# Both heads' probabilities in one tile: one softmax-sum addition for two heads, split anew between GpSimd and VectorE

## The chip, the cores and the metric

The kernel runs on one core of one Trainium2 chip. The time is the device time of one execution in microseconds (us). The engines are named as in the profile: PE is TensorE (PEld its weight loads), DVE is VectorE, ACT is ScalarE, POOL is GpSimd, SP is SyncE, from whose queue nearly all DMAs start.

## The reference

Four transformer layers in fp32 on one sequence of 2048 tokens with 128 features, each with an attention and a feed-forward part and residuals. The change lies in the attention of the second layer, L1, with 16 heads of 64 features:

```python
q = jnp.einsum('bsd,dhk->bshk', x, Wq) + bq
k = jnp.einsum('bsd,dhk->bshk', x, Wk) + bk
v = jnp.einsum('bsd,dhk->bshk', x, Wv) + bv
q = q / jnp.sqrt(jnp.asarray(depth, q.dtype))
attn = jnp.einsum('bqhd,bkhd->bhqk', q, k)
attn = jax.nn.softmax(attn, axis=-1)
out = jnp.einsum('bhqk,bkhd->bqhd', attn, v)
return jnp.einsum('bqhd,hdm->bqm', out, Wo) + bo
```

The queries are normalised tokens. Before it comes L0 (16 heads of 8 features, then a feed-forward part); after it come the L1 feed-forward, L2 (a three-neighbour attention and eight experts, one per token) and L3 (a recurrent memory in chunks of 64 tokens, then eight experts, two per token, and a shared one).

## The kernel before

**Order of work.** Every engine runs its instructions in the order in which the program issues them. That order is made while the program is built: `note` keeps a model clock for each engine, with costs per instruction from `COST`, and `fill` puts small pieces of the work of the other stages (`parts` and `helpers`, written as generators) between the steps of the attention, when the model says that their inputs and a PSUM bank are ready. `leave` is the number of banks that such pieces must leave free. Nothing is reordered on the chip, so an instruction that comes late delays all that stands behind it on its engine.

**L1 attention.** The queries are cut into five blocks (`QB`) of 512, 388, 512, 384 and 256 columns (some blocks carry four spare or extra columns). A *unit* is one block and one pair of heads, so there are 5 x 8 = 40 units, and a unit has 16 *steps*, one for each 128 keys. `l1_attn` runs over the 640 steps. In a step:

- TensorE makes the scores of both heads (four products for each, row halves side by side) into two PSUM banks of pool `st`, of which there are three. A score is already lessened by the row's maximum.
- ScalarE writes exp of each head's scores to an SBUF tile `P` of 128 x 512, from pool `pp` with seven buffers (two tiles in each step).
- `max_upto` issues the row maxima of a later unit: TensorE multiplies keys `km` by queries `qh` into banks of pool `mx` (five banks), VectorE reduces each (`mx<-mi`). These reductions run ahead of the unit that needs them. A unit of 512 columns has a pair of them in each step; smaller ones have fewer.
- `fill` puts in pieces of other stages: the preparation of queries, the ends of units, and, as soon as a block's result is there, L1's feed-forward, L2 and L3. They take their banks from pool `mx` too.
- `do_sum` handles the step before: it adds that step's P to a running sum over the steps, which is the softmax denominator before its sum over partitions. Steps 14 and 15 (`dve=(14, 15)`) go to VectorE (sum `acd`), steps 0 to 13 to GpSimd (sum `acg`). The first tile of either engine is only remembered; the second makes the sum with an addition of two P tiles. So each unit and head has 13 additions on GpSimd and one on VectorE.
- `do_pv` multiplies P by the values (`mi<-P,ka`), one bank for both heads over the 16 steps.

After a unit's last step, `do_merge` adds `acg` to `acd` on VectorE, once for each head, and `u_end` follows as a piece: TensorE sums over partitions (`mi<-acd,ones`), four DMAs turn the row of sums for a reciprocal and spread it back, VectorE multiplies the result `o` by it (`o<-o,rb`), and every second unit adds to the output projection. The next unit's sums take the same buffers (`l1a`, two for each of `acd` and `acg`, one for each head).

**After the attention** the rest of L2 and L3 is issued (`drain`). The experts of L3 run in two lanes and, from here on, in five more, which borrow the attention's tiles: `lane_tiles` takes weights into `acd`, `acg` and `ka` tiles, `lane_work` takes one P tile of pool `pp` for each expert step and uses its two halves of 256 columns. L0's attention uses pool `pp` too, with tiles of one head.

In the profile nearly every instruction has the line of the helper that records it, L147, so groups are told apart by their tiles.

Of the kernel before, what the change touches and what calls it, by code (L numbers as in the profile page):

```python
# [28 lines left out]
CH = 64  # L29
NCH = S // CH  # L30
ATANH = (1.0000000039388743, 0.3333315796754013, 0.20012426861749952, 0.13980709417165652, 0.14087328632693624)
T = dict(lead0=22, more0=4, mgap=0.4, pvq=2, lim0=0.5, fq=(3,), pl=-0.5, pr=1.0, tlow=2, tback=3, late=0.3, pvp="mx", mxp="mx", ex=(1280, 1792, 2047), low=1, lows='ge', keep=1, leave=2, pvn=1, sp=0, rdy=40., eu=2, qg=(22, 16, 10), em=2, el=6, sem=0.2, same=1.2, tsame=3.0, order="hdmBbAaEcCeg", ps=dict(st=3, mx=5), dma=2.3, slack=0.1, lim=0.3, backlog=2.5, lead=(10, 8, 6), pp=7, dve=(14, 15), qp=(1, 1), lanes=2, xl=5,
         QB=[(0, 512, 512), (512, 384, 388), (896, 512, 512), (1408, 384, 384), (1792, 256, 256)])


# [35 lines left out]
def body(ctx: ExitStack, tc: tile.TileContext, x, pa, pb, pc, pi, pd, pr, pr0, pe, pw, out):  # L71
# [87 lines left out]
    ctx.enter_context(tc.manual_schedule(engines={ET.PE, ET.DVE, ET.Activation, ET.Pool}))  # L159
    sm = ctx.enter_context(tc.tile_pool(name="sm", bufs=3))  # L160
    tp = ctx.enter_context(tc.tile_pool(name="tp", bufs=2))
    pp = ctx.enter_context(tc.tile_pool(name="pp", bufs=T["pp"]))

    bank = dict(st=[0.0] * 3, pv=[0.0], mx=[0.0] * 3, bg=[0.0])
    owner = {}
# [352 lines left out]
    l0ctx = ExitStack()  # L518
    l0 = l0ctx.enter_context(tc.tile_pool(name="l0", bufs=1))
    l0w = l0ctx.enter_context(tc.tile_pool(name="l0w", bufs=2))  # L520
    qd = dram.tile([16, 6, 8, S], BF16, name="qd")
    kd = dram.tile([16, 6, 8, S], BF16, name="kd")

# [148 lines left out]
    def l0_attn():  # L672
# [49 lines left out]
        for g in range(N):  # L722
            h, j = divmod(g, 16)
            i = h % NKQ
            if j == 0:
                need(("m0", h))
                need(("ld", h))
            if j == 2 and h + 2 < H0:
                helper(("ld", h + 2), l0_load(h + 2))
            pts = []  # L730
            pss = []
            for q in range(4):
                if q == T["pvq"] and prev is not None:
                    do_pv(*prev)
                if not pss:

                    while min(bank["st"]) > clk["T"] + T["mgap"] and min(bank["mx"]) < min(bank["st"]) - T["mgap"] and \
                            done[0] < min(4 * N, 4 * (g + LEAD + T["more0"]) + q):
                        more_max()

                    two = done[0] == 4 * N and h >= H0 - 2 and q % 2 == 0
                    for e in range(1 + two):
                        pss.append(take(["st"]))
                        r = slice(LOW * e, LOW * e + NR0P + 2)
                        mm(pss[e], kop[i][r, j * 128:(j + 1) * 128], qop[i][r, (q + e) * 512:(q + e + 1) * 512],
                           par=e and 0.02)
                    if done[0] < 4 * N and done[0] <= 4 * (g + LEAD) + q:
                        more_max()
                ps = pss.pop(0)
                p = pp.tile([128, 512], F32, name="P", tag="P")  # L750
                se.activation(p, ps, AF.Exp, scale=1.0 / math.sqrt(HD0))
                rel(ps)
                pts.append(p)
                fill(T["lim0"], "t" if q not in T["fq"] else "")
            prev = (g, pts)
            emitted.add(("s0", g))
            yield g
# [192 lines left out]
    e0ctx.close()  # L950
    psum_pools(**T["ps"])
    in0[0] = False
    leave[0] = T["leave"]
    COST.update(L1COST)
    clk.update(dict.fromkeys("TADPS", 0.0))
    for d in (wr, rd, by, bank):
# [4 lines left out]
    l1 = ctx.enter_context(tc.tile_pool(name="l1", bufs=1, reuse_waits="tile"))  # L961
    kap = ctx.enter_context(tc.tile_pool(name="kap", bufs=3, reuse_waits="tile"))
    l1w = ctx.enter_context(tc.tile_pool(name="l1w", bufs=2, reuse_waits="tile"))
    l1a = ctx.enter_context(tc.tile_pool(name="l1a", bufs=2, reuse_waits="tile"))
    KC = 256
    opool = ctx.enter_context(tc.tile_pool(name="opool", bufs=3, reuse_waits="tile"))
    def u_loadk(u, c):
# [8 lines left out]
    def u_end(u, o, accs):  # L976
# [3 lines left out]
        t = mi()  # L980
        if u == len(units) - 1:
            for e in range(2):
                mm(t[64 * e:64 * e + 64, :n], ones[:, 0:64], accs[e][:, :n], par=(e == 1))
            yield
            rb = l1w.tile([128, 512], F32, name="rb", tag="rb", bufs=1)
            ve.reciprocal(rb[:, :n], t[:, :n])
            rel(t)
            ve.tensor_tensor(o[:, :n], o[:, :n], rb[:, :n], ALU.mult)
            O[p] = o
            yield from stage_wo(qb, NP1 // 2 - 1)  # L990
            return
        for e in range(2):
            mm(t[32 * e:32 * e + 32, :n], ones[:, 0:32], accs[e][:, :n], tile_position=(0, 32 * e), par=(e == 1))
        emitted.add(("s", u))
        yield
        sr = l1w.tile([128, 512], F32, name="rb", tag="rb", bufs=1)
# [69 lines left out]
    def l1_attn():  # L1066
# [15 lines left out]
        def do_pv(g, pts, v):  # L1082
            u, k = divmod(g, 16)
            n = QB[units[u][0]][2]
            if k == 0:
                pv[u] = take([T["pvp"]])
            for e in range(2):
                mm(pv[u][64 * e:64 * e + 64, :n], v[:, k % SPC, 64 * e:64 * e + 64], pts[e][:, :n],
                   start=(k == 0), stop=(k == 15), par=(e == 1))
            if k == 15:  # L1090
                accs = acc.pop(u)
                if u:
                    need(("o", u - 1))
                o = opool.tile([128, 512], F32, name="o", tag="o")
                se.copy(o[:, :n], pv[u][:, :n])
                rel(pv.pop(u))
                ends.append((u, o, accs))

        def do_sum(g, pts, v):
            u, k = divmod(g, 16)  # L1100
            n = QB[units[u][0]][2]
            for e in range(2):
                a = acc.setdefault(u, [None, None])
                f = first.setdefault((u, e), {})
                eng, nm = (ve, "d") if k in T["dve"] else (ge, "g")
                if nm not in f:
                    f[nm] = [pts[e]]
                    continue
                if len(f[nm]) == 1:
                    if u:  # L1110
                        need(("s", u - 1), ("o", u - 1))
                    t = l1a.tile([128, 512], F32, name="ac" + nm, tag="ac" + nm)
                    eng.tensor_tensor(t[:, :n], f[nm][0][:, :n], pts[e][:, :n], ALU.add)
                    f[nm] = [t, 1]
                else:
                    t = f[nm][0]
                    eng.tensor_tensor(t[:, :n], t[:, :n], pts[e][:, :n], ALU.add)
                if k == 15:
                    a[e] = f["d"][0]
                    merge.append((f["d"][0], f["g"][0], n))  # L1120
                    del first[(u, e)]

        merge = []

        def do_merge():
            while merge:
                d, g_, n = merge.pop(0)
                ve.tensor_tensor(d[:, :n], d[:, :n], g_[:, :n], ALU.add)
            while ends:
                u, o, accs = ends.pop(0)  # L1130
                helper(("o", u), u_end(u, o, accs), max(wr[tname(t)] for t in accs))

        ends = []
        prev = []
# [1 line left out]
        for g in range(16 * U):  # L1136
# [15 lines left out]
            if k % SPC == 0:  # L1152
                ka, v = nxt.pop(0)
                g2 = g + 2 * SPC
                if g2 < 16 * U:
                    nxt.append(u_loadk(g2 // 16, (g2 % 16) // SPC))
            pts = []
            ks = slice((k % SPC) * 128, (k % SPC) * 128 + 128)
            pss = [take(["st"]) for _ in range(2)]
            ops = ((ka[:, 0, ks], qhh[u]), (ka[:, 0, ks], qlt[u % 2]), (ka[:, 1, ks], qhh[u]), (onr, mbt[u % 2]))  # L1160
            for i, (a, b) in enumerate(ops):
                for e in range(2):
                    rows = slice(64 * e, 64 * e + 64)
                    mm(pss[e][:, :n], a[rows], b[rows, :n], start=(i == 0), stop=(i == 3), par=e and 0.02)
            for e in range(2):
                pt = pp.tile([128, 512], F32, name="P", tag="P")
                se.activation(pt[:, :n], pss[e][:, :n], AF.Exp)
                rel(pss[e])
                pts.append(pt)
            max_upto(max_at(g + 16 + LEAD[n] + 1))  # L1170
            fill()
            if prev:
# [655 lines left out]
    def lane_tiles(lane):  # L1828
# [4 lines left out]
        if lane not in lane_bufs:  # L1833
            n = lane - LANES
            if n < 2:
                t = ("acd", "acg")[n]
                ws = [l1a.tile([128, 512], F32, name=t, tag=t)[:, :384] for _ in range(2)]
                r = l1x.tile([128, 512], F32, name="qf", tag="qf")
            else:
                t = kap.tile([128, 3, KC], F32R, name="ka", tag="ka").rearrange("p a b -> p (a b)").bitcast(F32)  # L1840
                ws = [t[:, :384], t[:, 384:768]]
                r = kmp.tile([128, 512], F32R, name="km", tag="km").bitcast(F32)
            lane_bufs[lane] = [(w.rearrange("p (a m) -> p a m", a=3), r[:, BN * i:BN * i + BN])
                               for i, w in enumerate(ws)]
# [3 lines left out]
    def lane_work(lane):  # L1848
        if lane < LANES:
            return bt(f"t3{lane}", 1), bt(f"te{lane}", 1)  # L1850
        p = pp.tile([128, 512], F32, name="P", tag="P")
        return p[:, :BN], p[:, BN:]

    def e_load(lane):

# [262 lines left out]
```

## Time and profile before

| What | Value |
|---|---|
| Three runs | 2988.46, 2989.47, 3006.5 us; median 2989.47 |
| Profiled execution | 3001.08 us, span of the profile 2999.2 us |
| Busy, share of the span | PE 92%, DVE 73%, ACT 53%, POOL 51% |
| Granted TensorE clock, mean | 0.936 |
| First L1 exponential, last one's end | 909 us, 2595 us |
| GpSimd additions `acg<-acg,P` and `acg<-P` | 960 and 80, 1011.4 and 91.1 us busy |
| VectorE additions `acd<-P`, merges `acd<-acd,acg` | 80 and 80 |
| VectorE maxima `mx<-mi`, L0 and L1 | 2080, 1322.1 us busy |

A line of the profile's groups names the engine, the operation, the tiles (result, arrow, inputs), the shape, the number of instructions, their busy time and mean, and the idle time of the engine before them with what ended it. The table by stage gives the busy time of every engine in a stretch. A timeline line has the start, the length and the instruction; equal instructions in a row are one line (x2, x4), and a bracket at the end is the idle time before it and what ended it. "mi" is a PSUM bank.

### The profile page before, as it was taken

How to read it: one execution, taken by the hardware profiler on the slowest of the kernel's cores; microseconds unless marked ns; L12 is line 12 of the kernel's file. 1: busy time of each engine (PE TensorE's matmuls, PEld its weight loads, DVE VectorE, ACT ScalarE, POOL GpSimd, SP SyncE). 2: the span in 40 equal slices, each digit the busy share in tenths (PEclk: the TensorE clock that was granted, in tenths of full speed). 3: DMA queues.
4: the chain of work that ended last, by engine and by line, in shares of the span. 5: the costliest groups of instructions: out<-in, count | busy, mean ns of one | idle time of the engine just before them, and what ended most of it. 6: DMA issues, size and time to landing. Idle time of an engine off the chain costs nothing.

```text
span 2999.2 us, 49776 instructions
## 1 busy us (share of the span) xinstructions
PE 2769.9 (92%) x16719; PEld 1307.0 (44%) x16719; DVE 2194.9 (73%) x4699; ACT 1582.9 (53%) x3933; POOL 1522.3 (51%) x1762
## 2 busy tenths in 40 slices
PE   7999999999979899999999999899989898888998
PEld 2222222322234344454444444455544555565666
DVE  7899898898534666566666778887677769787765
ACT  1788887888854444444444444444434334333444
POOL 2400110201127688866776876677767556443444
PEclk9999999999979999999999999999999999776779
DMA  6311231321144333433442332233334343312244
GB/s 142 72 28 22 72 84 17 101 54 46 53 141 135 92 112 110 121 110 111 138 119 87 94 95 87 89 105 108 109 97 114 108 117 94 88 52 61 76 104 115
DMA packets 247749, 275.80 MB, mean 92 GB/s; under 512 B 95747, under 2 KB 183330, under 8 KB 247366
## 3 DMA queue, kind: packets, MB, share of 16 engines
q1 hardware_dynamic: 246630, 272.43, 33.2%
q8 instruction: 132, 2.16, 0.3%
q14 instruction: 123, 1.01, 0.1%
q10 hardware_dynamic: 864, 0.20, 0.0%
HBM read 229.97 MB, written 42.28 MB: 91 GB/s over the span
## 4 chain that ended last, share of the span: by engine, by line
PE 70%; DVE 18%; ACT 6%; issue 3%; DMA 3%; POOL 1%; SPq 0%; ACTq 0%; DVEq 0%; POOLq 0%
PE mi L147 70%; DVE mx L147 5%; ACT P L147 3%; DVE sB L147 1%; DVE o L147 1%; DVE gq L147 1%; DMA ka<-kvd 1%; DVE gt L147 1%; DVE xs L147 1%; ACT kf L147 1%; ACT kh L147 1%; DVE xn L147 1%; DVE sG L147 1%; DVE acd L147 1%; DVE sA L147 0%
## 5 line engine op out<-in xcount | busy, mean ns | idle before, releaser
L147 DVE TENSOR_REDUCE mx<-mi 128x1 f32<-128x512 f32 (+1 forms) x2080 | 1322.1, 683 | 582.8 <-PE mi L147 571.5
L147 ACT ACTIVATE P<-mi 128x512 f32<-128x512 f32 (+3 forms) x2304 | 1137.0, 551 | 1004.1 <-PE mi L147 973.2
L147 POOL TENSOR_TENSOR acg<-acg,P 128x512 f32<-128x512 f32 (+3 forms) x960 | 1011.4, 1083 | 181.8 <-ACT P L147 180.0
L147 PE MATMUL mi<-P,ka 128*64 128x512 f32 (+3 forms) x2560 | 597.6, 546 | 2.3 <-DVE mx L147 2.3
L147 PE MATMUL mi<-qh,ka 64*128 64x512 f32 (+3 forms) x2560 | 521.0, 406 | 9.7 <-DMA ka<-kvd 6.8
L147 PEld LDWEIGHTS mi<-qh,ka 64*128 64x128 f32 x2560 | 247.0, 189 | 382.5 <-issue 347.0
L147 PE MATMUL mi<-kop,qop 48*128 48x512 bf16 x1024 | 348.6, 405 | 24.5 <-DVE mx L147 12.1
L147 PE MATMUL mi<-qop,kop 50*128 50x512 bf16 x1024 | 317.8, 391 | 27.1 <-ACT P L147 24.7
L147 PE MATMUL mi<-P,vop 128*32 128x512 f32 x2048 | 304.3, 623 | 13.9 <-ACT P L147 13.9
L147 POOL TENSOR_SCALAR vep<-mv 128x2 f32<-128x2 f32 (+1 forms) x24 | 5.5, 229 | 495.6 <-DVE mv L147 495.6
L147 PE MATMUL mi<-km,qh 64*128 64x512 f32 x1024 | 225.6, 410 | 30.4 <-DVE mx L147 23.8
L147 PE MATMUL mi<-mbt,onr 64*128 64x512 f32 (+3 forms) x1280 | 228.7, 351 | 1.5 <-DMA mbt<-mb 1.5
L147 PE MATMUL mi<-ql,ka 64*128 64x512 f32 (+3 forms) x1280 | 229.2, 353 | 0.0
L147 PEld LDWEIGHTS mi<-P,ka 128*64 128x64 f32 x2560 | 129.2, 137 | 225.3 <-issue 195.1
L147 PEld LDWEIGHTS <-kop 50*128 50x128 bf16 x1024 | 63.6, 95 | 304.9 <-issue 281.6
L147 POOL TENSOR_TENSOR acg<-P 128x512 f32<-128x512 f32 (+3 forms) x80 | 91.1, 1158 | 202.5 <-DVE acd L147 162.0
L147 PEld LDWEIGHTS mi<-km,qh 64*128 64x128 f32 x1024 | 107.1, 189 | 60.5 <-DVE mx L147 38.5
L147 PEld LDWEIGHTS mi<-mbt,onr 64*128 64x128 f32 x1280 | 124.6, 190 | 13.9 <-DMA mbt<-mb 2.2
L147 PEld LDWEIGHTS mi<-ql,ka 64*128 64x128 f32 x1280 | 125.7, 192 | 0.0
L147 PEld LDWEIGHTS <-qop 48*128 48x128 bf16 x1024 | 72.9, 96 | 97.2 <-issue 82.7
L147 PEld LDWEIGHTS mi<-P,vop 128*32 128x32 f32 x2048 | 55.5, 109 | 119.8 <-issue 90.7
L147 POOL TENSOR_TENSOR kl<-kf,kh 128x512 f32<-128x512 f32 x32 | 40.9, 1278 | 110.9 <-ACT kh L147 82.4
(509 smaller groups left out, 3464.4 us busy)
## 6 DMA issues: line engine op xcount, KB each, us to landing
ka<-kvd SPq DMA_DIRECT2D x320, 384.0 KB
km<-khd SPq DMA_DIRECT2D x159, 256.0 KB
khd<-kh SPq DMA_DIRECT2D x32, 256.0 KB
kvd<-kh SPq DMA_DIRECT2D x32, 256.0 KB
kvd<-kl SPq DMA_DIRECT2D x32, 256.0 KB
kvd<-vt SPq DMA_DIRECT2D x16, 512.0 KB
ka<-in_pw_dram SPq DMA_DIRECT2D x37, 192.0 KB
w3s<-in_pw_dram SPq DMA_DIRECT2D x35, 192.0 KB
```

Of the source, the lines that this page charges most:

```text
L147: r = f(*a, **k)
```

## The change

One P tile now holds both heads of a step, 128 x 2 x 512, from a new pool of five buffers. ScalarE still writes each head with an instruction of its own, and TensorE still reads each head by itself. `do_sum` makes one addition over both heads, of twice the columns, and so does the merge; the sums are one tile for both heads (pool `l1a`, one buffer of each). VectorE takes steps 5, 6, 11 and 12 of a unit and GpSimd the other twelve, so a unit has 11 additions on GpSimd and three on VectorE, and one merge. L0 keeps its tiles of one head in a pool of its own that ends with L0. The number of banks that pieces leave free is one more from the end of a unit's P-by-values product to the start of the next. The lanes take the new tiles: five P buffers where there were seven, and halves of one `acd` or `acg` tile where there were two tiles.

```diff
-T = dict(lead0=22, ..., pp=7, dve=(14, 15), ...
+T = dict(pp1=5, lead0=22, ..., pp=7, dve=(5, 6, 11, 12), ...
...
-    pp = ctx.enter_context(tc.tile_pool(name="pp", bufs=T["pp"]))
...
+    l0p = l0ctx.enter_context(tc.tile_pool(name="l0p", bufs=T["pp"]))
...
-                p = pp.tile([128, 512], F32, name="P", tag="P")
+                p = l0p.tile([128, 512], F32, name="P", tag="P")
...
-    leave[0] = T["leave"]
+    leave[0] = T["leave"] + 1
...
-    l1a = ctx.enter_context(tc.tile_pool(name="l1a", bufs=2, reuse_waits="tile"))
+    l1a = ctx.enter_context(tc.tile_pool(name="l1a", bufs=1, reuse_waits="tile"))
+    pp = ctx.enter_context(tc.tile_pool(name="pp", bufs=T["pp1"], reuse_waits="tile"))
...
-            mm(t[32 * e:32 * e + 32, :n], ones[:, 0:32], accs[e][:, :n], tile_position=(0, 32 * e), par=(e == 1))
+            mm(t[32 * e:32 * e + 32, :n], ones[:, 0:32], accs[:, e, :n], tile_position=(0, 32 * e), par=(e == 1))
...
             if k == 0:
                 pv[u] = take([T["pvp"]])
+                leave[0] -= 1
...
-                mm(pv[u][64 * e:64 * e + 64, :n], v[:, k % SPC, 64 * e:64 * e + 64], pts[e][:, :n],
+                mm(pv[u][64 * e:64 * e + 64, :n], v[:, k % SPC, 64 * e:64 * e + 64], pts[:, e, :n],
...
                 rel(pv.pop(u))
+                leave[0] += 1
...
         def do_sum(g, pts, v):
             u, k = divmod(g, 16)
             n = QB[units[u][0]][2]
-            for e in range(2):
-                ...
-                    t = l1a.tile([128, 512], F32, name="ac" + nm, tag="ac" + nm)
-                    eng.tensor_tensor(t[:, :n], f[nm][0][:, :n], pts[e][:, :n], ALU.add)
-                ...
+            f = first.setdefault(u, {})
+            eng, nm = (ve, "d") if k in T["dve"] else (ge, "g")
+            if nm not in f:
+                f[nm] = [pts]
+            elif len(f[nm]) == 1:
+                if u:
+                    need(("s", u - 1), ("o", u - 1))
+                t = l1a.tile([128, 2, 512], F32, name="ac" + nm, tag="ac" + nm)
+                eng.tensor_tensor(t[:, :, :n], f[nm][0][:, :, :n], pts[:, :, :n], ALU.add)
+                f[nm] = [t, 1]
+            else:
+                t = f[nm][0]
+                eng.tensor_tensor(t[:, :, :n], t[:, :, :n], pts[:, :, :n], ALU.add)
+            if k == 15:
+                acc[u] = f["d"][0]
+                merge.append((f["d"][0], f["g"][0], n))
+                del first[u]
...
-                ve.tensor_tensor(d[:, :n], d[:, :n], g_[:, :n], ALU.add)
+                ve.tensor_tensor(d[:, :, :n], d[:, :, :n], g_[:, :, :n], ALU.add)
...
+            pts = pp.tile([128, 2, 512], F32, name="P", tag="P")
             for e in range(2):
-                pt = pp.tile([128, 512], F32, name="P", tag="P")
-                se.activation(pt[:, :n], pss[e][:, :n], AF.Exp)
+                se.activation(pts[:, e, :n], pss[e][:, :n], AF.Exp)
...
-                ws = [l1a.tile([128, 512], F32, name=t, tag=t)[:, :384] for _ in range(2)]
+                t = l1a.tile([128, 2, 512], F32, name=t, tag=t)
+                ws = [t[:, e, :384] for e in range(2)]
...
-        p = pp.tile([128, 512], F32, name="P", tag="P")
-        return p[:, :BN], p[:, BN:]
+        p = pp.tile([128, 2, 512], F32, name="P", tag="P")
+        return p[:, 0, :BN], p[:, 0, BN:]
```

More of the change, by code (lines that the diff above doesn't have):

```diff
@@ L31 @@
 ATANH = (1.0000000039388743, 0.3333315796754013, 0.20012426861749952, 0.13980709417165652, 0.14087328632693624)
-T = dict(lead0=22, more0=4, mgap=0.4, pvq=2, lim0=0.5, fq=(3,), pl=-0.5, pr=1.0, tlow=2, tback=3, late=0.3, pvp="mx", mxp="mx", ex=(1280, 1792, 2047), low=1, lows='ge', keep=1, leave=2, pvn=1, sp=0, rdy=40., eu=2, qg=(22, 16, 10), em=2, el=6, sem=0.2, same=1.2, tsame=3.0, order="hdmBbAaEcCeg", ps=dict(st=3, mx=5), dma=2.3, slack=0.1, lim=0.3, backlog=2.5, lead=(10, 8, 6), pp=7, dve=(14, 15), qp=(1, 1), lanes=2, xl=5,
+T = dict(pp1=5, lead0=22, more0=4, mgap=0.4, pvq=2, lim0=0.5, fq=(3,), pl=-0.5, pr=1.0, tlow=2, tback=3, late=0.3, pvp="mx", mxp="mx", ex=(1280, 1792, 2047), low=1, lows='ge', keep=1, leave=2, pvn=1, sp=0, rdy=40., eu=2, qg=(22, 16, 10), em=2, el=6, sem=0.2, same=1.2, tsame=3.0, order="hdmBbAaEcCeg", ps=dict(st=3, mx=5), dma=2.3, slack=0.1, lim=0.3, backlog=2.5, lead=(10, 8, 6), pp=7, dve=(5, 6, 11, 12), qp=(1, 1), lanes=2, xl=5,
          QB=[(0, 512, 512), (512, 384, 388), (896, 512, 512), (1408, 384, 384), (1792, 256, 256)])
@@ L982, in u_end @@
             for e in range(2):
-                mm(t[64 * e:64 * e + 64, :n], ones[:, 0:64], accs[e][:, :n], par=(e == 1))
+                mm(t[64 * e:64 * e + 64, :n], ones[:, 0:64], accs[:, e, :n], par=(e == 1))
             yield
@@ L1101, in do_sum @@
             n = QB[units[u][0]][2]
-            for e in range(2):
[L1103 to L1111, printed above, removed]
-                    t = l1a.tile([128, 512], F32, name="ac" + nm, tag="ac" + nm)
-                    eng.tensor_tensor(t[:, :n], f[nm][0][:, :n], pts[e][:, :n], ALU.add)
[L1114 to L1121, printed above, removed]
+            f = first.setdefault(u, {})
[15 more added lines that the diff above has]
+                del first[u]
         merge = []
@@ L1127, in do_merge @@
                 d, g_, n = merge.pop(0)
-                ve.tensor_tensor(d[:, :n], d[:, :n], g_[:, :n], ALU.add)
+                ve.tensor_tensor(d[:, :, :n], d[:, :, :n], g_[:, :, :n], ALU.add)
             while ends:
                 u, o, accs = ends.pop(0)
-                helper(("o", u), u_end(u, o, accs), max(wr[tname(t)] for t in accs))
+                helper(("o", u), u_end(u, o, accs), wr[tname(accs)])
         ends = []
@@ L1156, in l1_attn @@
                     nxt.append(u_loadk(g2 // 16, (g2 % 16) // SPC))
-            pts = []
             ks = slice((k % SPC) * 128, (k % SPC) * 128 + 128)
@@ L1164, in l1_attn @@
                     mm(pss[e][:, :n], a[rows], b[rows, :n], start=(i == 0), stop=(i == 3), par=e and 0.02)
+            pts = pp.tile([128, 2, 512], F32, name="P", tag="P")
             for e in range(2):
-                pt = pp.tile([128, 512], F32, name="P", tag="P")
-                se.activation(pt[:, :n], pss[e][:, :n], AF.Exp)
+                se.activation(pts[:, e, :n], pss[e][:, :n], AF.Exp)
                 rel(pss[e])
-                pts.append(pt)
             max_upto(max_at(g + 16 + LEAD[n] + 1))
```

## The prediction, made before the result was known

> **What bounds the kernel now.** I read the page first, for the shares; then busy time by stage, cutting the span at the first exponentials of each block of queries in the L1 attention (909 to 2595 us: 40 units of 16 steps, with blocks of 512, 388, 512, 384 and 256 columns); then the waits inside those stages; then the timelines where TensorE stood still.
>
> ```profile
> PE 2769.9 (92%) x16719; PEld 1307.0 (44%) x16719; DVE 2194.9 (73%) x4699; ACT 1582.9 (53%) x3933; POOL 1522.3 (51%) x1762
> ```
> ```profile
> core 0: us, PE busy (x) PEld busy (x) DVE busy (x) ACT busy (x) POOL busy (x), PEclk, DMA share, GB/s
> 909.00:1248.00 339.00, 330.12 (x1858) 142.99 (x1857) 199.21 (x301) 160.51 (x303) 271.08 (x236) 0.98 0.36 111
> 1248.00:1543.00 295.00, 290.21 (x1928) 147.15 (x1928) 189.69 (x347) 139.57 (x340) 213.58 (x216) 0.99 0.41 122
> 1543.00:1939.00 396.00, 376.62 (x2066) 169.56 (x2066) 307.46 (x556) 174.27 (x392) 289.64 (x250) 0.98 0.30 92
> 1939.00:2281.00 342.00, 326.22 (x2151) 171.92 (x2148) 246.18 (x519) 148.19 (x422) 235.78 (x273) 0.97 0.37 105
> 2281.00:2595.00 314.00, 283.96 (x2120) 162.85 (x2117) 243.94 (x608) 125.42 (x473) 191.63 (x292) 0.91 0.42 110
> 2595.00:2999.00 404.00, 344.46 (x1723) 256.64 (x1721) 289.38 (x1069) 160.11 (x660) 167.20 (x279) 0.76 0.31 79
> ```
>
> The first columns are the stretch and its length. TensorE sets the pace: in the five L1 stages it lacks only 8.9, 4.8, 19.4, 15.8 and 30.0 us of being always busy, 78.9 us in all. That is all that the change can win there. The engine it relieves, POOL, is not the bound; the engine it loads, DVE, is busy for 59, 64, 78, 72 and 78% of the stages.
>
> What makes the 78.9 us shows in one place:
>
> ```profile
> 971.82 10.90 DVE L147 TENSOR_TENSOR o<-o,rb 128x512 f32<-128x512 f32 x1
> ```
> ```profile
> 967.38 14.79 POOL L147 TENSOR_TENSOR acg<-acg,P 128x512 f32<-128x512 f32 x12
> ```
> ```profile
> 984.20 0.58 PE L147 MATMUL mi<-ident,m 128*4 128x128 f32 x2 [8.88 <-DVE m L147]
> ```
>
> A DVE product of two SBUF tiles, 0.66 us at its shortest, stays open for 10.90 us, until POOL's unbroken row of additions ends; the maxima queue behind it, and TensorE stands for 8.88 us. I followed each held DVE instruction of the five stages in the timelines of DVE and POOL. At the end of a POOL instruction with a pause after it, however short, DVE always got in (67 of 67); at an end with the next addition already running, 144 times of 208. TensorE's gaps behind single holds of over 2 us (o, gq, u, cc, sA) add up to 33.9 us.
>
> **What goes and comes, engine by engine.** The sums are against the profiled execution, 3001.08 us with a span of 2999.2, which is 0.4% above the median of the runs, 2989.47; I put the difference on the median.
>
> ```profile
> L147 POOL TENSOR_TENSOR acg<-acg,P 128x512 f32<-128x512 f32 x384 | 489.7, 1311 | 51.2 <-ACT P L147 51.0
> ...
> L147 POOL TENSOR_TENSOR acg<-acg,P 128x256 f32<-128x256 f32 x192 | 137.4, 738 | 57.4 <-ACT P L147 56.8
> ...
> L147 POOL TENSOR_TENSOR pbl<-vt,pbh 128x1024 fp32r<-128x1024 f32 x2 | 4.7, 2362 | 0.0
> ```
> ```profile
> L147 DVE TENSOR_TENSOR o<-o,rb 128x512 f32<-128x512 f32 x16 | 32.6, 2039 | 0.9 <-DMA rb<-rcd 0.8
> ...
> L147 DVE TENSOR_TENSOR acd<-P 128x512 f32<-128x512 f32 x32 | 20.6, 683 | 0.0
> ```
>
> POOL: 26 additions a unit (960 + 80, 1102 us) become 11 double ones, 440. A 1024-column POOL addition isn't in the trace; it costs 2.36 us by the 1024-column subtraction, 2.62 by twice the 512-column row. I take 2.36, the same number of columns, and by the line from there to 738 ns, 1.84, 1.82 and 1.28 us for 388, 384 and 256: 16x11x2.36 + 8x11x(1.84 + 1.82 + 1.28) = 850 us. POOL gives up some 250 us and has two breaks of two steps a unit, so its unbroken rows shrink from 26 additions to four double ones. **Gain 1:** the long holds. Bounds 0 and -33.9; a hold of one double addition remains, so I take two thirds, **-23**.
>
> ACT: the exponentials stay as many. Their waits for a free P tile (POOL acg) are 19.7 us in 14 times; ten half tiles instead of seven end most. TensorE waits for ACT P 21.5 us in these stages (17.7 at weight loads, 3.8 at products), for several reasons. Bounds 0 and -10; **-5**.
>
> DVE: two additions and two merges a unit become three additions and one merge, all double. With 685 ns at 512 and 405 at the shortest 256, 1024 columns take 1.24 us, 776 and 768 0.97 and 0.96, 512 0.69. Per unit 2.2, 1.7, 1.5 and 0.9 us more (512, 388, 384, 256): 69 us. The additions of steps 6 and 12 come as POOL starts again:
>
> ```profile
> 1216.59 1.08 ACT L147 ACTIVATE P<-mi 128x512 f32<-128x512 f32 x2 [1.10 <-PE mi L147]
> ...
> 1216.82 1.29 DVE L147 TENSOR_REDUCE mx<-mi 128x1 f32<-128x512 f32 x2 [1.08 <-PE mi L147]
> 1217.33 8.69 POOL L147 TENSOR_TENSOR acg<-acg,P 128x512 f32<-128x512 f32 x7 [0.45 <-ACT P L147]
> ```
>
> POOL starts 0.20 us after an exponential's end (1216.59 + 0.54 = 1217.13). With both heads in one tile that is 1.08 + 0.20 = 1.28 us after the pair's start. DVE's sum of the step before stands in its queue behind this step's two maxima, so it is free at 0.23 + 1.29 = 1.52 us. POOL is first by 0.24 us, with step 7 or 13, and DVE waits until 1.28 + 2.36 = 3.64, for 2.1 us. At 388 and 384 the same arithmetic gives 1.4 us in the three steps of four that have a pair of maxima, at 256 0.5 in half: 32x2.1 + 24x1.4 + 8x0.5 = 105 us. Step 11 finds POOL idle. Behind the waiting addition stand the next maxima and small operations of L2 and L3; TensorE waits for both, for the PSUM banks of the first and the results of the second.
>
> The price is read from the stages. From the two with DVE at 59 and 64% (PE short by 0 without the 8.88, and 1.6%) to the three at 72 to 78% (4.6 to 9.6%) PE's loss grows by about 0.39 us for each us of DVE time. DVE gains 51, 30, 51, 29 and 12 us in the five stages, which makes 20, 12, 20, 11 and 5 us. In the first two, DVE idles 1.06 to 1.10 us in each step, waiting for TensorE, and little is queued behind it, so I take 4 of the 32; in the others all 36. **+40**, bounds 0 (DVE's idle, 437.6 us of waits for TensorE in these stages, covers everything) and +68.
>
> The Trainium skill's page "SBUF — State Buffer" (section "Who interferes with whom") speaks against the change: a DVE instruction with two SBUF inputs contends with a GpSimd instruction that reads SBUF, and what starts second is fully blocked until the first finishes. The rows above agree that it blocks, but 10.90 us is some nine additions, not one. By the rule alone there would be no long holds to gain from, and the sum would be 23 us higher.
>
> Unit end: the merge now waits for POOL's step 15 instead of 13. Two double steps of POOL end 0 to 0.9 us after DVE's maxima, and the next maxima and the helpers stand behind it.
>
> ```profile
> 1209.20 1.28 DVE L147 TENSOR_TENSOR acd<-P 128x512 f32<-128x512 f32 x2
> ...
> 1210.40 1.29 DVE L147 TENSOR_TENSOR acd<-acd,acg 128x512 f32<-128x512 f32 x2
> ```
>
> But 2.57 us of DVE work at that place become 1.24. I cost it at **0**: the 1.33 us removed cover the wait; with POOL later than that, 40 x 0.4 us, so 0 to +16. No DMA is added; the four that carry the sums follow the merge as before, and SP's queue is passed by nothing. The reserve of one more bank while no product bank is held lasts one step a unit: 0.
>
> The tail after 2595: seven P buffers become five for the five extra lanes. A P tile is taken every 2.6 us (276 products read one, two to a tile: 138 tiles in 354 us), and the first lives some 9 us (written from 2641.3, read by a product at 2650.3), less than 5 x 2.6. **+3**, bounds 0 and +15.
>
> Sum: -23 - 5 + 40 + 0 + 3 = **+15 us**: 3016 for the profiled execution, **3004 us** beside the median of before.
>
> **Rivals.** *Faster, 2950.* DVE's idle hides the additions and the holds vanish: -34 - 10 + 5 = -39. For it: the first two stages lose next to nothing at 59 and 64%. Against: DVE at 78% in the third is to take 51 us more.
>
> *Slower, 3078: the additions starve.* If POOL's double addition takes longer than a tight step (maxima of 1216.82 and 1219.20: 2.38 us apart), POOL doesn't pause between steps 7 to 10 or 13 to 15, and a DVE addition that misses the first end may be held for the row, 9.3 or 7.0 us, as o was. That hold's gap was 2.0 us shorter than the hold: (8.2 + 1.2 - 2.0) = 7.4 us each. With 64 of 208 ends missed, 32 x 0.31 x 7.4 = 73 us above the forecast. My price, 2.36, is just under the step and the other, 2.62, over it; 2.38 is the point that decides. For it: those two prices. Against: 67 of 67 at pauses.
>
> *Slower, about 3032: DVE is the bound.* All 68 us and 15 of the tail, less the 28 gained and 12 of the merge's wait added: +67 at most, a middle of +43. For it: units at 85 to 91% of DVE exist in the third stage.
>
> **From cases to numbers.** Forecast 45%, faster rival 18%, starved additions 18%, DVE-bound 19%. About 1% is what a measurement here tells from no change: so within 1% 0.45, faster 0.18, slower 0.37. The range leaves out a tenth on each side: 2950 to 3062.
>
> **What would show it.** Right: 440 POOL additions of 2.3 to 2.5 us at 1024; DVE additions far over 1.24 us at steps 6 and 12 and near it at 11; DVE share up by 8 to 13 points at 512; no hold near 10 us. Wrong: DVE additions near 1.24 us throughout, or PE losing under 60 us between the first and last L1 exponential (a gain); holds of 7 to 9 us on acd (starved); a tail well over 404 us.

## The result: 0.9% slower, and the profile after

Fifteen runs of the changed kernel have a median of 3022.0 us, fifteen of the kernel before 3000.41; the ratio is 1.0088, 95% interval 1.007 to 1.0106, or about 26 us. Forecast were 15 us. The profiled execution took 3022.61 us, with a span of 3020.9, so it stands for the median.

The changed kernel's busy times and then its stages (the stretch, its length, busy us of PE, PEld, DVE, ACT and POOL, TensorE's granted clock, DMA), cut at the same exponentials as before:

```profile
PE 2790.0 (92%) x16719; PEld 1314.2 (44%) x16719; DVE 2357.7 (78%) x4700; ACT 1576.3 (52%) x3932; POOL 1330.3 (44%) x1161
```
```profile
907.60:1245.00 337.40, 332.93 (x1855) 143.55 (x1855) 252.38 (x304) 158.56 (x302) 228.93 (x116) 0.99 0.36 111
1245.00:1536.30 291.30, 290.09 (x1926) 147.04 (x1924) 226.51 (x346) 138.31 (x339) 179.91 (x97) 1.00 0.41 123
1536.30:1955.30 419.00, 388.31 (x2036) 173.42 (x2035) 343.84 (x516) 171.54 (x366) 242.92 (x125) 0.95 0.29 86
1955.30:2311.70 356.40, 336.49 (x2167) 176.26 (x2165) 285.08 (x560) 150.72 (x445) 201.21 (x158) 0.95 0.35 101
2311.70:2626.00 314.30, 287.80 (x2161) 166.05 (x2159) 249.15 (x628) 125.03 (x486) 157.51 (x173) 0.92 0.39 104
2626.00:3021.00 395.00, 338.83 (x1696) 251.57 (x1692) 282.13 (x1050) 157.66 (x650) 166.15 (x280) 0.77 0.34 85
```

The third stage grew by 22 us (397 to 419) and the fourth by 15 (342 to 356); the first two lost 5 together, the fifth kept its length, the tail lost 9. The first two stages took far more DVE time (199 to 252, 190 to 227 us) and did not suffer: little other work stands behind it there.

Hardly any of the growth is TensorE standing still for longer. Length less PE busy, added up over the five stages, is 82.8 us; it was 78.9. The other 29 of the 33 us by which the L1 attention grew are busy time, of nearly as many products (10134, before 10106), at a lower granted clock: 0.98 became 0.95 in the third stage and 0.97 became 0.95 in the fourth. Busy time times clock is 369 us in the third stage of both kernels. What a stop does can be seen in the kernel before, around the one of 8.88 us: the same four products before and behind it, and the stage columns around it.

```profile
972.87 1.08 PE L147 MATMUL mi<-P,ka 128*64 128x512 f32 x4
...
984.71 1.98 PE L147 MATMUL mi<-P,ka 128*64 128x512 f32 x4
```
```profile
945.00:965.00 20.00, 20.00 (x114) 8.70 (x112) 12.72 (x22) 10.44 (x19) 13.35 (x30) 1.00 0.31 94
...
985.00:990.00 5.00, 5.00 (x22) 1.87 (x21) 1.61 (x3) 1.28 (x3) 0.71 (x1) 0.69 0.24 79
990.00:1005.00 15.00, 15.00 (x88) 6.45 (x84) 9.59 (x17) 8.07 (x15) 7.95 (x7) 1.00 0.36 104
```

In the 5 us behind the stop the clock is 0.69, and the products take nearly twice as long. There the stop cost more than its own length. How much of the lower clock of whole stages comes from stops was not measured apart.

The groups of GpSimd and VectorE additions, and one of VectorE's held ones in the timelines of DVE and POOL:

```profile
L147 POOL TENSOR_TENSOR acg<-acg,P 128x1024 f32<-128x1024 f32 x160 | 408.9, 2555 | 228.3 <-ACT P L147 210.4 <-ACT thm L147 7.3 <-ACT xtm L147 3.7
...
L147 POOL TENSOR_TENSOR acg<-P 128x1024 f32<-128x1024 f32 x16 | 37.7, 2359 | 32.9 <-ACT P L147 18.1 <-DVE acd L147 14.9
```
```profile
L147 DVE TENSOR_TENSOR acd<-acd,P 128x1024 f32<-128x1024 f32 x32 | 59.0, 1844 | 0.0
L147 DVE TENSOR_TENSOR acd<-P 128x1024 f32<-128x1024 f32 x16 | 52.1, 3258 | 0.1
```
```profile
1050.93 1.29 DVE L147 TENSOR_REDUCE mx<-mi 128x1 f32<-128x512 f32 x2 [0.95 <-PE mi L147]
1052.13 3.31 DVE L147 TENSOR_TENSOR acd<-P 128x1024 f32<-128x1024 f32 x1
```
```profile
1051.99 2.37 POOL L147 TENSOR_TENSOR acg<-acg,P 128x1024 f32<-128x1024 f32 x1 [4.22 <-ACT P L147]
```

`acd<-P` is step 6, and all 16 of them at 1024 columns took 2.92 us or more. `acd<-acd,P` mixes steps 11 and 12; taken apart in order of time, step 11 has a mean of 1.22 us and step 12 of 2.47, with 11 of 16 held. The timeline shows why: POOL, after a pause of 4.22 us, starts step 7 at 1051.99; DVE comes out of the maxima at 1052.13, 0.14 us too late, and waits for all of it.

### The profile page after: what moved, and what is told of

It reads as the page before. It is cut to its first block, busy times and chain, and to the rows that moved or that the text cites. A ratio compares the mean times of both kernels' runs of the same rounds, so it can differ in the third digit from the quotient of the medians.

```text
span 3020.9 us, 48034 instructions
## 1 busy us (share of the span) xinstructions
PE 2790.0 (92%) x16719; PEld 1314.2 (44%) x16719; DVE 2357.7 (78%) x4700; ACT 1576.3 (52%) x3932; POOL 1330.3 (44%) x1161
## 4 chain that ended last, share of the span: by engine, by line
PE 65%; DVE 21%; ACT 6%; DMA 3%; issue 3%; POOL 1%; SPq 0%; ACTq 0%; POOLq 0%; DVEq 0%
PE mi L147 65%; DVE mx L147 7%; ACT P L147 3%; DVE acd L147 3%; DVE sB L147 1%; DMA ka<-kvd 1%; DVE xs L147 1%; ACT kf L147 1%; DVE gt L147 1%; DVE xn L147 1%; DVE o L147 1%; DVE ql L147 1%; POOL acg L147 1%; DMA km<-rwd 1%; ACT kh L147 1%
## 5 line engine op out<-in xcount | busy, mean ns | idle before, releaser
L147 POOL TENSOR_TENSOR acg<-acg,P 128x1024 f32<-128x1024 f32 (+3 forms) x400 | 824.7, 2062 | 521.0 <-ACT P L147 472.2
L147 PE MATMUL mi<-km,qh 64*128 64x512 f32 x1024 | 239.7, 417 | 42.5 <-DVE mx L147 35.1
L147 POOL TENSOR_TENSOR acg<-P 128x1024 f32<-128x1024 f32 (+3 forms) x40 | 77.5, 1938 | 80.5 <-ACT P L147 49.9
L147 DVE TENSOR_TENSOR acd<-acd,P 128x1024 f32<-128x1024 f32 (+3 forms) x80 | 110.3, 1379 | 0.3
```

Source lines behind the costliest of these rows:

```text
L147: r = f(*a, **k)
```

## The experiments

Three theories. **A**: VectorE's additions come late (65 us of new work, 80 us of waiting for GpSimd), and TensorE waits for what stands behind them. **B**: GpSimd's instructions, now twice as long, hold every small two-input VectorE instruction of the other layers for longer, whatever the new additions do. **C**: the bank reserve and the new order of the other layers' pieces. Ratios are to the kernel before, run on the same chip beside each.

**1. VectorE's addition ahead of the maxima.**

```diff
+            early = prev and prev[-1][0] % 16 in T["dve"]
+            if early:
+                do_sum(*prev[-1])
             max_upto(max_at(g + 16 + LEAD[n] + 1))
             fill()
-            if prev:
+            if prev and not early:
                 do_sum(*prev[-1])
```

> The changed kernel with one difference: VectorE's addition of a step is issued ahead of the next step's maxima instead of behind them, so that it is in VectorE's queue before GpSimd's next addition starts. Theory A (VectorE's additions are late: 69 us of work and 78 us of waiting for GpSimd, and TensorE waits for what stands behind them): step 6 at 1024 columns falls from 3.26 us to about 1.2, step 12 from 2.47 to about 1.2, and about half of the loss goes: ratio to before near 1.004. Rival B (GpSimd's instructions of twice the length hold every small VectorE instruction longer, whatever the additions do): the additions shorten too, but the ratio stays near 1.009. Rival C (the order of the other stages' pieces and the bank reserve): stays near 1.009 too.

Measured: ratio 1.0016 (0.9988 to 1.0043). In the timeline of DVE the addition of step 6 now comes before the maxima and is not held:

```profile
1048.24 1.17 DVE L147 TENSOR_TENSOR acd<-P 128x1024 f32<-128x1024 f32 x1
1049.33 1.28 DVE L147 TENSOR_REDUCE mx<-mi 128x1 f32<-128x512 f32 x2
```

The waiting of the additions falls from 80 us to 10, and 0.7% goes with it, more than the half expected. That supports A. Its profiled execution took 3027 us and the median of its runs is 3010, so its stages are not used alone.

**2. Pair tiles, but steps 14 and 15 for VectorE.** `dve=(14, 15)` in the changed kernel.

> The changed kernel with the old choice of steps: both heads in one tile and one addition, but VectorE takes steps 14 and 15, GpSimd the other fourteen (13 double additions a unit). Theory A: VectorE's work is that of before and its additions meet no GpSimd addition, so the loss goes: ratio 0.998 to 1.003. Rival B: GpSimd has more double additions than in the change (520 against 440) in rows of 13, so the small instructions of VectorE are held longer still: ratio 1.01 or more. Rival C: as the change, 1.009.

Measured: 1.0097 (1.0057 to 1.0136). VectorE's additions are never held (1.22 us each at 1024 columns) and its work is less than before, and yet the loss is all there. A alone is refuted. B forecast this (1.01 or more, just above the value measured); C's 1.009 fits as well.

**3. Tiles of one head, but the new steps.** `dve=(5, 6, 11, 12)` in the kernel before.

> The kernel before with the new choice of steps alone: tiles and additions of one head, VectorE adds steps 5, 6, 11 and 12. Theory A: VectorE's work grows by some 80 us (eight instructions of one head a unit instead of four) and its additions meet GpSimd's, each held at most one or two single additions of 1.27 us: ratio 1.005 to 1.010. Rival B: GpSimd has fewer additions (880) of the old length, with breaks: ratio 0.995 to 1.000. Rival C: no reserve is changed: near 1.000.

Measured: 0.999 (0.9964 to 1.0015). The additions are held as in the change, 83 us in all (1.43 us at step 6 for 512 columns, 0.68 alone), and this costs nothing net; the small instructions of other layers are held for 135 us instead of 177. The new steps alone are neutral; that is B's range, at its upper end, and C's value.

**4. A reduction in the place of VectorE's addition.** As many elements, one SBUF input.

```diff
...
-                eng.tensor_tensor(t[:, :, :n], t[:, :, :n], pts[:, :, :n], ALU.add)
+                if nm == "d":
+                    ve.tensor_reduce(rsum[u], pts[:, :, :n], AX.X, ALU.add)
+                else:
+                    eng.tensor_tensor(t[:, :, :n], t[:, :, :n], pts[:, :, :n], ALU.add)
...
```

The addition that begins VectorE's sum is replaced alike, and the merge adds the reduction's result to GpSimd's sum.

> The changed kernel with VectorE's three additions a unit replaced by a reduction of the same P tile (as many elements, one SBUF input, so that it should not wait for GpSimd); it leaves out the sums of steps 5, 6, 11 and 12. It keeps the work and takes the waiting away. Theory A: the reductions take 1.1 to 1.3 us at 1024 columns in all three steps, ratio near 1.004, between none and the whole loss. If the waiting is all of the loss: 1.000; if the work is all of it: 1.008. Rival B and C: near 1.009.

Measured: 1.0025 (1.0003 to 1.0048). The group of the reductions, all three steps in one line:

```profile
L147 DVE TENSOR_REDUCE acr<-P 128x2 f32<-128x1024 f32 x48 | 58.0, 1209 | 0.0
```

None of the 120 took over 1.22 us. The work remains, the waiting is gone, and 0.6% with it: the waiting of the additions costs some 20 us, by this and by experiment 1.

This run also gives a comparison in which the order of the other work stays as it was. VectorE's other instructions come in the same order as in the change for the first 1531 of 2193, and ScalarE's for the first 1406 of 1938. The stretches from the first L1 exponential to there, the change first, then number 4:

```profile
907.55:2269.45 1361.90, 1306.94 (x7699) 619.25 (x7699) 1070.84 (x1654) 600.74 (x1401) 823.58 (x473) 0.97 0.35 103
```
```profile
907.69:2239.09 1331.40, 1288.38 (x7699) 613.44 (x7699) 995.46 (x1653) 600.52 (x1401) 783.58 (x474) 0.98 0.37 105
```

Both hold 7699 products of TensorE, and VectorE's other instructions are held alike (152 and 149 us). The sum's instructions on VectorE take 210 us in one and 134 in the other, and number 4 is there 30.5 us earlier, 0.40 us for each us of waiting; 12 of these are idle time of TensorE and 19 busy time. Behind that point the orders part, and at the end of L1 number 4 is ahead by 15 us. These are single executions.

**5. The old reserve of banks.** Without `+ 1` and without the two lines that move `leave[0]`.

> The changed kernel with the reserve of PSUM banks of the kernel before (two throughout). Theory A (late additions of VectorE) and B (GpSimd's double additions hold small VectorE instructions): nothing to do with it, ratio to before 1.006 to 1.011, as the change. Rival C (the reserve, and with it the order of the other stages' pieces): the loss goes, 1.000 to 1.003.

Measured: 1.0083 (1.006 to 1.0105), as the change. The reserve is no cause; the rest of C, the new order, is not tested by this.

**6. GpSimd's additions one head at a time**, in the same pair tiles:

```diff
...
-                eng.tensor_tensor(t[:, :, :n], t[:, :, :n], pts[:, :, :n], ALU.add)
+                for s_ in parts_of(nm):
+                    eng.tensor_tensor(t[:, s_, :n], t[:, s_, :n], pts[:, s_, :n], ALU.add)
...
```

Here `parts_of` gives (0, 1) for GpSimd and both heads at once for VectorE; the addition that begins a sum is treated alike.

> The changed kernel with each GpSimd addition of two heads made as two additions of one head; tiles, pools, reserve, steps and VectorE's double additions stay. Theory B (the length of GpSimd's instructions is the loss): the ratio falls to that of single tiles with the new steps, 0.997 to 1.002; VectorE's additions at step 6 are held 0.9 us instead of 2.1. If the pools, the reserve or the lanes' five buffers are the loss (C): 1.006 to 1.011. Theory A alone (only the waiting of VectorE's additions): 1.003 to 1.006, as part of that waiting stays.

Measured: 0.9931 (0.9909 to 0.9953), lower than any theory had it. The edit changes only the length of GpSimd's instruction, and the kernel is 1.6% faster than the change; tiles, pools and the lanes' buffers are the change's, so they are not the loss. But the planner makes the order anew: VectorE's other instructions part from the change's order after 251 of 2193. The same groups as above:

```profile
L147 DVE TENSOR_TENSOR acd<-P 128x1024 f32<-128x1024 f32 x16 | 27.2, 1698 | 0.1
```
```profile
L147 POOL TENSOR_TENSOR acg<-acg,P 128x512 f32<-128x512 f32 x320 | 445.1, 1423 | 182.7 <-ACT P L147 182.7
```

GpSimd is busier than in the change and the kernel is faster. The additions are held for 27 us instead of 80, the other instructions for 123 instead of 208: not fewer of them (168 and 177), but shorter, 0.73 us each instead of 1.17.

**7 and 8. The addition first, with tiles of one head (7) and with experiment 6 (8).**

> Tiles of one head as before, VectorE adds steps 5, 6, 11 and 12, and its additions are issued ahead of the next step's maxima. Theory A: the additions take 0.68 us at 512 columns (they took 1.43 at step 6 in the run of single tiles with the new steps), and the kernel is faster than before: 0.990 to 0.996. Theory B: single additions already held little; 0.997 to 1.000.

> The changed kernel with both edits: GpSimd's additions one head at a time, VectorE's double additions ahead of the maxima. A and B both: if the two costs add up, this has neither and is faster than before, 0.990 to 0.997. If they are one cost told twice, it is as good as the better of the two alone. C: 1.002 or more, as the run with the sum first had.

Measured: 0.9875 (0.9856 to 0.9894) and 0.9776 (0.9751 to 0.9801). Both edits to the change together bring it from 1.0088 to 0.9776, 3.1%; alone they brought 0.7 and 1.6%. Together is more than the sum, so it is not one cost told twice. Between numbers 1 and 8 the additions wait little in both (10 and 3 us) and GpSimd's length alone is edited: 2.4%. Both numbers are below their forecast ranges, and not all of that is the two costs: of the 63 us between the profiles of 6 and 8, 47 lie in the tail, behind the L1 attention. Number 8, the change with GpSimd in two and the sum first, beats both kernels; its median is 2938.11 us.

**9 and 10. GpSimd in four, and the old steps, both in the version of experiment 8.** In 9 each head's columns are halved once more; 10 has `dve=(14, 15)`.

> As the run with GpSimd's additions in two and the sum first (ratio 0.978), but each GpSimd addition in four, half a head's columns each. GpSimd works about a quarter longer on them (four times some 0.73 us at 512 columns against two times 1.27). If the length of the single instruction is what holds VectorE's small instructions (B): the mean hold falls below the 0.76 us of that run, to 0.4 to 0.5, and the ratio is 0.970 to 0.980. If the share of the time that GpSimd holds counts more than the length: holds as long in total, ratio 0.980 to 0.995. If GpSimd becomes late itself (11 x 2.9 us of a unit's 40): 0.99 or more.

> As the run with GpSimd's additions in two and the sum first, but VectorE adds steps 14 and 15, as in the kernel before; GpSimd's single additions are then those of the kernel before in number and length. It asks what the new steps are worth once neither cost is there. If their gain is the breaks in GpSimd's rows: long holds come back (several over 5 us) and the ratio is 0.990 to 1.003, near before. If the gain comes from the pair tile, its five buffers and the one merge: 0.975 to 0.985.

Measured: 0.9863 (0.9832 to 0.9894) and 1.0211 (1.018 to 1.0243). In 9 the holds do get shorter, 82 us instead of 148: those of up to 2.5 us have a mean of 0.43 us, against 0.64 in 8, and with the longer ones it is 0.60, where 0.4 to 0.5 was forecast. The L1 attention is the shortest of all, but the tail is 35 us longer than in 8; the ratio is outside the range that B gave. The 1.0211 of 10 is outside both of its ranges. In 10 the long holds are back, eight over 5 us against one in 8. One of them, DVE, POOL and PE:

```profile
1154.19 8.32 DVE L147 TENSOR_TENSOR o<-o,rb 128x512 f32<-128x512 f32 x1
```
```profile
1149.62 12.34 POOL L147 TENSOR_TENSOR acg<-acg,P 128x512 f32<-128x512 f32 x10
```
```profile
1163.17 0.79 PE L147 MATMUL mi<-km,qh 64*128 64x512 f32 x1 [5.39 <-DVE mx L147]
```

Behind that one hold TensorE stands for 5.39 us. But 10 also has a tail of 475 us, 80 more than the change: 2026 of TensorE's products are left for it, against 1696 in the change and 1706 in 8. Number 2, with the same steps and GpSimd additions of twice the length, is 1.1% faster than 10, although its small holds are longer (1.10 us on average against 0.64). So what the order leaves for the tail can outweigh shorter holds.

**All together.** From each profile: the length of the L1 attention, the tail behind it, and how long VectorE was held. A hold is what a DVE instruction without a PSUM input takes over the shortest of its kind, counted from 0.25 us; the sum additions include the merges.

| Kernel | L1, us | tail, us | held: sum additions | held: others | holds over 2.5 us | ratio |
|---|---|---|---|---|---|---|
| before | 1686 | 404 | 2 | 177 | 10 | 1 |
| the change | 1718 | 395 | 80 | 208 | 1 | 1.0088 |
| 1 sum first | 1725 | 393 | 10 | 207 | 0 | 1.0016 |
| 2 pair, 14 and 15 | 1720 | 407 | 0 | 219 | 2 | 1.0097 |
| 3 single, new steps | 1696 | 407 | 83 | 135 | 8 | 0.999 |
| 4 reduction | 1703 | 396 | 2 | 202 | 1 | 1.0025 |
| 5 old reserve | 1730 | 402 | 78 | 205 | 3 | 1.0083 |
| 6 GpSimd in two | 1668 | 420 | 27 | 123 | 6 | 0.9931 |
| 7 single, sum first | 1670 | 399 | 10 | 124 | 5 | 0.9875 |
| 8 in two, sum first | 1654 | 373 | 3 | 148 | 7 | 0.9776 |
| 9 in four, sum first | 1637 | 408 | 13 | 82 | 7 | 0.9863 |
| 10 in two, 14 and 15 | 1677 | 475 | 0 | 157 | 10 | 1.0211 |

The holds of other instructions follow the length of GpSimd's instruction: those of up to 2.5 us have a mean of 0.43 us with at most 256 columns (number 9), 0.63 to 0.70 with 512 (before, 3, 6, 7, 8, 10) and 1.10 to 1.16 with 1024 (the change, 1, 2, 4, 5). The length of the L1 attention roughly follows the sum of both columns of holds: 95 us in number 9, with 1637 us, to 288 in the change, with 1718, or 0.42 us of L1 for each us held, an estimate from these two. These are single executions, a kernel's runs spread by some 10 us to either side, and numbers 1 to 4, held alike for 204 to 219 us, lie between 1696 and 1725. Nor is the same work in every L1 attention: 9803 products in number 10, 10018 to 10165 in the others. The tail follows no column. It holds whatever the planner did not place inside the L1 attention, 1663 to 2026 products at a granted clock of 0.75 to 0.83, and that differs from order to order.

## Why the prediction was right, and where it was not

**The size and the place** were right: within 1%, slower, the loss in the third and fourth stages and none in the first two. That the sum came so near is in part luck. In the profiles the L1 attention was to grow by 12 us and grew by 33; the tail was to grow by 3 and lost 9.

**What the loss is made of** was not seen. The prediction reads it as idle time of TensorE, calls the 78.9 us of it "all that the change can win there", and prices VectorE's time in it. The idle time was to grow by 12 us and grew by 4; most of the loss is busy time at a lower clock. Nor are gains idle time alone: in number 8 the L1 attention is 32 us shorter than before with as many products (10124), and 18 of these are idle time.

**The race at steps 6 and 12** was right in its mechanism and nearly in its numbers: at step 6 a 1024-column addition was to take 1.24 + 2.1 us and took 3.26; step 11 was to be free and took 1.22. All holds of the additions were to be 105 us and were 80, since at 384 columns and at step 12 fewer lost the race. The new work was to be 69 us: the `acd` instructions take 239.9 us where they took 94.7, which without the 80 is 65. VectorE's share at 512 columns was to rise by 8 to 13 points; it rose by 16 in the first stage and by 4 in the third, which itself grew.

**Gain 1, -23 us, was the step that failed.** The long holds did vanish, ten over 2.5 us to one. But the sum of what the other instructions were held rose, from 177 us to 208: the long ones gave back 44 us, and the ordinary ones, of up to 2.5 us, took 75 more, since each grew with GpSimd's instruction (193 of 0.66 us on average before, 176 of 1.15 us after). The prediction saw "a hold of one double addition remains" only for the few long ones and forgot that nearly two hundred short ones grow likewise. At 0.42 us for each us held the term is about +13, an estimate, not -23. The prediction's own price of VectorE's time, 0.39 us per us, would have given +12; it was not applied to this term. That price itself is not confirmed: the 0.40 of number 4 and the 0.42 are near it, but they are the length of L1 for each us of waiting, not idle time of TensorE, and for the new work no run has a price. Number 4, with that work and without the waiting, loses 0.25% in all, some 7.5 us.

**The tail** was costed at +3 and is 9 us shorter; more of the other layers' work was done inside a longer L1 attention (1696 of TensorE's products are left for the tail, before 1723). Five buffers do no harm that shows. That made up for part of the failed gain.

**ACT's waits for P tiles**, 19.7 us before on POOL's additions, are 3.1 us after, as expected. **The merge** was to wait 0 to 0.9 us a unit; it waits for POOL 8.0 us in all, in ten units. Nothing is lost there.

**The rivals.** The starved additions didn't happen. The deciding point was a double addition of 2.38 us, and it is 2.36 where nothing disturbs it, so in the L1 attention POOL has a pause behind 372 of 438 additions (before, 227 of 1040), most often for the next P:

```profile
ACT P L147 <- PE mi L147: 885.3, 606, 8.6
POOL acg L147 <- ACT P L147: 522.1, 177, 10.4
DVE mx L147 <- PE mi L147: 314.7, 230, 7.5
```

In this view (who waits for whom: us, times, longest) POOL's waits for P grew from 191.6 us to 522.1. At all 192 ends of a POOL instruction with a pause behind it a held DVE instruction got in, and at 38 of 52 without one. The faster rival was wrong about this kernel, but its condition, that nothing is held, came nearest to true in number 9 (95 us held, ratio 0.9863). The third rival, VectorE as the bound with +43 us, is wrong in its form: the first two stages took 53 and 37 us more of VectorE's time and did not grow. The measured +26 lies between the forecast and it.

The Trainium skill's rule ("SBUF — State Buffer", "Who interferes with whom"), that the one to issue first has the shared pair of SBUF ports for its whole instruction and the other is fully blocked, fits each hold of the additions in the change; 14 of 52 ends missed and the 8.32 us above show again that it may be several instructions, not one. The same section says that a VectorE reduction never contends on trn2, and experiment 4's 120 reductions agree.

**What stays open.** Why number 8 beats number 7 by 1% with nearly as many us held, and why the planner leaves the tails of 8, 9 and 10 as they are: 373, 408 and 475 us, with 1706, 1784 and 2026 products at clocks of 0.82, 0.80 and 0.79. The order of the other layers' pieces changes with each edit, and no run here keeps it fixed to the end. For the waiting of the additions number 4 has a stretch of fixed order. The 1.6% for GpSimd's length is measured as a whole; how much of it came by way of the order was not tried apart.

## What to carry to other kernels

Joining two GpSimd instructions into one saves little time on GpSimd (2.36 us against two of 1.27) and here raised what a small VectorE instruction is held, on average, from 0.63 us (number 6) to 1.15 (the change, holds of up to 2.5 us); count the waiting instructions on the other engine before joining, and keep GpSimd's pieces short while VectorE is on the path. Leave breaks in GpSimd's rows (one hold over 5 us in number 8 with them, eight in number 10 without), and issue VectorE's additions where GpSimd is still waiting for its data: here that was one line's place ahead of two maxima. A stage's price of delay (TensorE time lost per us of VectorE time) can be estimated from a profile's stages, but idle time alone leaves out what the clock loses, and the price must be applied to every term that delays VectorE. Where a planner makes the order anew, compare the work left for the tail before a gain is put down to the edit.

## What was not expected of the hardware

A GpSimd that is busier can make the kernel faster: the additions `acg` are 992 us of busy time in experiment 6 and 902 in the change (POOL in all 1413.5 and 1330.3 us), and experiment 6 is 1.6% quicker. At step 6 GpSimd's lead of 0.14 to 0.54 us (under 0.16 in 12 units) decides over 1.7 to 2.1 us of waiting, and it does so in each of the 16 units of 512 columns.
